# Dense row tiles of a two-layer graph kernel: eight by f32 matmuls, or ten by three bf16 parts

## The chip, the cores and the metric

The kernel runs on one core of one Trainium2 chip. The metric is the device time of one execution, in microseconds (us); a kernel's time is the median over its runs. The engines are named as the profile names them: PE (TensorE), DVE (VectorE), ACT (ScalarE), POOL (GpSimd) and SP (SyncE, which here only issues transfers). Each engine works through a queue of its own, in order. PSUM, into which PE accumulates, has eight banks of 128 x 512 f32 words; SBUF holds everything else that is on the core.

## The reference

`x` is 4096 x 512 in f32, `adj` a symmetric 0/1 matrix of 4096 x 4096 with ones on its diagonal and about nine in a row. Layer 0 is an attention in which every head takes the value of its best neighbour; layer 1, to which the change belongs, takes a mean over neighbours:

```python
def _L1_gnn_ref(x, adj, W_self, b_self, W_nb, b_nb, W_comb, b_comb):
    mask = (adj > 0).astype(x.dtype)
    deg = jnp.sum(mask, axis=1, keepdims=True)
    agg = mask @ x / jnp.maximum(deg, 1.0)
    self_f = x @ W_self + b_self
    nb_f = agg @ W_nb + b_nb
    combined = jnp.concatenate([self_f, nb_f], axis=-1)
    out = combined @ W_comb + b_comb
    return jax.nn.relu(out)

h = jnp.maximum(_layernorm(x, axis=-1), 0.0)
x = x + _L0_gnn_ref(h, adj, L0_gnn_WQ, ...)
h = jnp.maximum(_layernorm(x, axis=-1), 0.0)
x = x + _L1_gnn_ref(h, adj, L1_gnn_W_self, ...)
```

Matrices may be moved across the mean: with G = h · (W_nb · lower half of W_comb), a row's neighbour part is the sum of the rows of G that its mask picks, over its degree.

## The kernel before

`adj` is so sparse that the kernel turns it into lists. The first stage (to about 300 us) reads it, packs each row into bit words and computes keys and values. The rows are then sorted by degree into 32 tiles of 128 rows, the largest degrees first; `CAPS` gives the length of the lists in each tile (24, 15, 14, 13, 12, 12, 12, 11 | 11, 11, 10, ... 5), one entry of which is the row itself. `sidx` holds the lists, `perm` the place of each sorted row in the output. Should a list not fit, a flag (`fi`) makes the program run a general path afterwards; with these inputs it doesn't.

The middle stage goes through the tiles in 32 turns (`turns`, to about 905 us): attention, the second normalisation, and for each tile the row's own share (`X1_d`, rows of x and y) and its rows of G, stored to `G_d` by SP. Beside that, 105 one-hot rows are made here, one for each neighbour slot of the first DENSE = 8 tiles (`hots`): ACT makes each in two instructions (L1517, L1518) from codes that DVE computes (L1498), PE adds them up with the identity (`hot_product`), and `words_turn` turns each finished tile and stores it in `W_d` (L1549). The sum has, for row q and column c of 0 to 255, a word whose bit s says whether q has the neighbour 256·s + c; so one word covers the 16 planes of 256 rows of G. At the last turn `wT` is loaded with these words, 8 x 256 of 4 bytes in each partition (L1664). After the turns, ACT works off `owed_out` for rows owed from the middle stage and the tail.

The last stage, from the first gather of `G_d`, is what the change rewrites. It has two kinds of tiles.

Dense tiles, 0 to 7: PE multiplies masks with all 4096 rows of G, and each tile has a PSUM bank (`dacc`) to itself. For plane s, `dense_keys` (L1797) loads 256 rows of G into `gk` through SP, `dense_mask` (L1556) has DVE shift the words by 30 - s and keep bit 30, so that a neighbour reads 2.0 in f32 and all else 0, and `dense_sum` (L1805) issues 16 f32 matmuls of 128 x 512. The mask is made in two instructions, for seven tiles and for one; there are three mask buffers. The factor 2.0 is taken out by `half`, half of the reciprocal degree.

Sparse tiles, 8 to 31: for each neighbour slot POOL issues an indirect DMA that gathers 128 rows of `G_d` into `room` (L1121), n = CAPS - 1 for a tile, 174 in all. `room` is used as a ring of three tiles (L1863). DVE adds up the n rows in one tensor_reduce (`total`, L1830), for the last tile by pairwise additions (`halved`, L1839).

Either way `finish` follows: L1820 computes y + sum / degree, L1821 relu and x + that, two DVE instructions; y and x come from `X1_d` through SP, four tiles ahead (`load_x1`, L1813 and L1815). Then POOL stores the 128 rows to their places with an indirect DMA (`put_rows`, L1137); if two stores follow one another, a small memset (`gap`, L1136) goes between. The last stage's stores are issued one tile late: a tile's gathers come first, then the store of the tile before.

The order on all engines is the order of the code here (`manual_schedule`). The loop over sparse tiles counts POOL's calls, and plane s's mask, the load of keys s + 1 and the matmuls are issued once `calls >= pace * s - 7`, with `pace = 11`. The last three planes are issued together, tile by tile, so that the dense tiles become final one after another; `finish` of dense tiles 0 to 2 follows tile 29's, 3 to 5 tile 30's, and 6 and 7 stand ahead of the last sparse tile's:

```python
for k in (range(6, DENSE) if r == KT - 1 else ()):
    finish(k, dacc[k], half[:, k : k + 1], x1s.pop(k))
acc = (total if r < KT - 1 else halved)(gg, n)
finish(r, acc, smeta[:, r, M_RD - M_DEG : M_RD + 1 - M_DEG], x1s.pop(r))
for k in {KT - 3: range(0, 3), KT - 2: range(3, 6)}.get(r, ()):
    finish(k, dacc[k], half[:, k : k + 1], x1s.pop(k))
```

Of the kernel before, what the change touches and what calls it, by code (L numbers as in the profile page):

```python
# [9 lines left out]
F32 = mybir.dt.float32  # L10
BF16 = mybir.dt.bfloat16
I32 = mybir.dt.int32
# [6 lines left out]
P = 128  # L19
D = 512  # L20
# [497 lines left out]
GMAX = 10  # L518
DENSE = 8
# [25 lines left out]
def sparse_path(  # L545
# [14 lines left out]
    W_d = dram.tile([DENSE, P, 2, P], I32, tag="W_d", name="W_d")  # L560
# [550 lines left out]
    with ExitStack() as pb:  # L1111
# [379 lines left out]
        def word_codes(r):  # L1491

            n = CAPS[r] - 1
            code = bp.tile([P, 3, LIST], F32, tag="code", name="code")[:, :, 0:n]
            of = sidx[:, ds(sat[r] + 1, n)]
            ci = code[:, 2, :].bitcast(I32)
            nc.vector.tensor_scalar(ci, of, SEG - 1, None, ALU.bitwise_and)
            nc.vector.tensor_scalar(code[:, 0, :], ci, float(-STEEP), None, ALU.mult)  # L1498
            nc.vector.tensor_scalar(ci, of, 8, None, ALU.logical_shift_right)
            nc.vector.tensor_scalar(  # L1500
                code[:, 1, :].bitcast(I32), ci, float(2**23), float(127 * 2**23), ALU.mult, ALU.add
            )
            st[r]["code"] = code
# [35 lines left out]
        def words_turn():  # L1539

            for r, k, acc in summed:
                if k < CAPS[r] - 2:
                    continue
                pt = pst.tile([P, NC, P], F32, tag="tr", name="tr")
                for h in range(2):
                    nc.tensor.transpose(pt[:, h, :], st[r]["wg"][:, ts(h, P)], ident)
                wi = bp.tile([P, 2, P], I32, tag="wst", name="wi", bufs=1)
                nc.scalar.copy(wi, pt[:, 0:2, :])
                nc.sync.dma_start(W_d[r], wi)  # L1549
            summed.clear()  # L1550

        def dense_mask(s):

            mk = mks[s % 3]
            for a, b in ((0, DENSE - 1), (DENSE - 1, DENSE)):
                nc.vector.tensor_scalar(  # L1556
                    mk[:, a:b].rearrange("p r h q -> p r (h q)").bitcast(I32), wT[:, a:b, 0:SEG],
                    30 - s, 0x40000000, ALU.logical_shift_left, ALU.bitwise_and,
                )
            masks[s] = mk  # L1560
# [91 lines left out]
        for i in range(-5, KT):  # L1652
# [9 lines left out]
            if i == KT - 1:  # L1662
                wT = wp.tile([P, DENSE, SEG + 2], I32, tag="w_a", name="wT")
                nc.sync.dma_start(  # L1664
                    wT[:, :, 0:SEG], W_d.rearrange("r p h q -> p r (h q)")
# [110 lines left out]
        mks = [gp.tile([P, DENSE, 2, P], F32, tag="kg", name="mk") for _ in range(2)]  # L1776
# [6 lines left out]
    with ExitStack() as pd:  # L1783
# [5 lines left out]
        dacc = [psd.tile([P, D], F32, tag=f"da{r}", name="da") for r in range(DENSE)]  # L1789
        keys = {}  # L1790
        mks.append(kp.tile([P, DENSE, 2, P], F32, tag="mk", name="mk", bufs=1))
# [8 lines left out]
        def dense_sum(*planes):  # L1800
            todo = [(s, h, r) for s in planes for h in range(2) for r in range(DENSE)]
            if len(planes) > 1:
                todo.sort(key=lambda shr: shr[2])
            for s, h, r in todo:
                nc.tensor.matmul(  # L1805
                    dacc[r], masks[s][:, r, h, :], keys[s][:, h, :],
                    start=(s == 0 and h == 0), stop=(s == NPL - 1 and h == 1),
                )

        def load_x1(r):  # L1810
            x1 = dp.tile([P, 2, D], F32, tag="x1", name="x1", bufs=DENSE + 6)
# [14 lines left out]

        def total(g, n):

            acc = kp.tile([P, D], F32, tag="acc", name="acc", bufs=2)
            nc.vector.tensor_reduce(  # L1830
                acc, g[:, 0:n, :].rearrange("p n f -> p f n"), AX.X, ALU.add
            )
            return acc
# [16 lines left out]
        ahead, late3 = 2, NPL - 3  # L1850
        for s in range(ahead + 1):
            dense_keys(s)
        for s in range(ahead):
            dense_sum(s)
        s = ahead
        calls = 0

        pace = 11
        x1s = {}
        for r in range(DENSE, KT):  # L1860
            n = CAPS[r] - 1
            for q in [*range(r, min(r + 4, KT)), *(range(DENSE) if r == KT - 6 else ())]:
# [25 lines left out]
        assert s == NPL  # L1888
# [50 lines left out]
```

## Time and profile before

| | us |
|---|---|
| median of 3 runs (lowest, highest) | 1190.85 (1189.97, 1191.04) |
| the profiled execution | 1188.29 |
| its span, first to last instruction | 1186.5 |
| busy in the span: PE / DVE / ACT / POOL | 1023.9 / 982.7 / 550.1 / 715.1 |

The busy time of the engines in stretches of the last stage, with the TensorE clock that was granted in each (1.00 is full speed):

| stretch, us | PE | DVE | ACT | POOL | clock |
|---|---|---|---|---|---|
| 905 to 934 | 28.53 | 9.00 | 7.67 | 21.75 | 1.00 |
| 934 to 1000 | 65.80 | 60.89 | 0.15 | 50.25 | 1.00 |
| 1000 to 1060 | 60.00 | 57.70 | 0.00 | 45.68 | 1.00 |
| 1060 to 1122 | 56.44 | 55.62 | 0.00 | 47.37 | 1.00 |
| 1122 to 1151 | 28.37 | 26.06 | 0.00 | 20.86 | 0.89 |
| 1151 to 1173 | 12.60 | 20.29 | 0.00 | 16.33 | 0.84 |
| 1173 to 1186.5 | 0.00 | 0.00 | 0.00 | 0.00 | 0.50 |

A POOL busy time is that of the instructions themselves; the pause between two DMA issues is not in it. A group's line in the profile gives line, engine, operation, output and inputs, shape and count, then busy time and mean duration in ns, then the idle time before these instructions and what ended most of it. A timeline's line gives start, duration, engine, line, operation, operands and, in brackets, the wait before it and what ended that.

### The profile page before, as it was taken

To read this page: it belongs to the slowest core of one execution; us is meant where nothing else is said; L and a number is where in the kernel's file an instruction comes from. 1 tells how busy PE (TensorE), PEld (TensorE's weight loads), DVE (VectorE), ACT (ScalarE), POOL (GpSimd) and SP (SyncE) were. 2 spreads that over 40 slices of the span, in tenths; PEclk is the share of its full clock that TensorE was granted. 3 is DMA by queue.
4 is the path that set the end of the run, shared out by engine and by line. 5 is a ranking of instruction groups with operands and counts; after the bars stand their busy time and mean duration, and the time that the engine had idled before them with its cause. 6 is when DMAs were issued, how large, how long until landed. Compare 5 with 4: busy or idle time off the path is not lost. (4 is left out here: it accounts for less than half of the span.)

```text
span 1186.5 us, 11454 instructions
## 1 busy us (share of the span) xinstructions
PE 1023.9 (86%) x3079; PEld 501.6 (42%) x3079; DVE 982.7 (83%) x1548; ACT 550.1 (46%) x1222; POOL 715.1 (60%) x939
## 2 busy tenths in 40 slices
PE   3999999979599668688879989888989999999792
PEld 1555555644244224344334434444434444444340
DVE  4358789889289798798989999999983699998894
ACT  3777777932222377486567678754462100000000
POOL 3332323312677757757777777777713777777774
PEclk9999999989799878889889889888999999999996
DMA  9999999979797678889898889988865888888973
GB/s 353 418 420 418 413 418 375 396 226 293 229 269 251 180 233 261 255 278 292 281 289 281 284 280 298 291 279 280 284 256 171 306 310 275 321 288 276 369 242 108
DMA packets 115594, 348.44 MB, mean 294 GB/s; under 512 B 21472, under 2 KB 23552, under 8 KB 107328
## 3 DMA queue, kind: packets, MB, share of 16 engines
q0 software_dynamic: 60560, 201.01, 53.0%
q1 hardware_dynamic: 50560, 146.56, 32.5%
q10 hardware_dynamic: 4400, 0.05, 0.3%
q8 instruction: 26, 0.43, 0.1%
q14 instruction: 48, 0.39, 0.1%
HBM read 287.75 MB, written 64.00 MB: 296 GB/s over the span
## 5 line engine op out<-in xcount | busy, mean ns | idle before, releaser
L1805 PE MATMUL da<-gk,mk 128*128 128x512 f32 x512 | 223.2, 599 | 6.9 <-DVE mk L1556 6.2
L1121 POOL DMA_INDIRECT room<-G_d,sidx x174 | 168.5, 969 | 84.6 <-issue 80.7
L636 PE MATMUL q<-wq,hqT 128*128 128x512 f32 x256 | 151.0, 745 | 51.3 <-DVE pr L1244 51.3
L1250 DVE TENSOR_REDUCE sc<-pr 128x32 f32<-128x2048 f32 (+3 forms) x114 | 183.3, 1608 | 3.8
L1121 POOL DMA_INDIRECT kg<-K_d,sidx x161 | 153.4, 953 | 49.0 <-issue 40.2
L1830 DVE TENSOR_REDUCE acc<-room 128x512 f32<-128x4096 f32 (+5 forms) x23 | 153.0, 6651 | 32.5 <-DMA room<-G_d,sidx 30.6
L1805 PEld LDWEIGHTS da<-gk,mk 128*128 128x128 f32 x512 | 98.2, 192 | 131.9 <-issue 123.1
L1121 POOL DMA_INDIRECT room<-K_d,sidx x118 | 111.6, 945 | 42.9 <-issue 25.6
L1121 POOL DMA_INDIRECT o<-K_d,vi x112 | 108.1, 965 | 34.2 <-issue 32.0
L636 PE MATMUL pk<-wk,room 128*128 128x512 f32 x256 | 118.5, 606 | 2.6 <-ACT room L821 2.6
L636 PE MATMUL pv<-wv,room 128*128 128x512 f32 x256 | 112.6, 592 | 0.0
L636 PEld LDWEIGHTS q<-wq,hqT 128*128 128x128 f32 x256 | 59.2, 243 | 123.0 <-issue 77.7
L1244 DVE TENSOR_TENSOR pr<-q,kg 128x2048 f32<-128x2048 f32 (+3 forms) x47 | 93.3, 1985 | 11.2 <-DMA kg<-K_d,sidx 10.1
L1393 PE MATMUL pr<-swS,hT 128*128 128x512 f32 x216 | 97.1, 592 | 0.0
L636 PE MATMUL pg<-swN,hT 128*128 128x512 f32 x216 | 97.1, 593 | 0.0
L760 ACT ACTIVATE mkt<-adjt,sgb 128x2048 bf16<-128x2048 int32 x44 | 88.0, 1999 | 2.1 <-POOL adjt L678 2.1
L1244 DVE TENSOR_TENSOR pr<-q,room 128x2048 f32<-128x2048 f32 (+3 forms) x42 | 73.2, 1744 | 18.1 <-DMA room<-K_d,sidx 16.0
L636 PEld LDWEIGHTS pv<-wv,room 128*128 128x128 f32 x256 | 48.3, 190 | 59.3 <-issue 59.1
L636 PEld LDWEIGHTS pk<-wk,room 128*128 128x128 f32 x256 | 47.5, 196 | 51.5 <-issue 47.8
L830 DVE SCALAR_TENSOR_TENSOR ks<-pk,swe 128x512 f32<-128x512 f32 x32 | 21.9, 686 | 52.5 <-PE pk L636 46.8
L1517 ACT ACTIVATE hot<-ramp,code 128x256 bf16<-128x256 bf16 x105 | 52.5, 500 | 22.5 <-DVE code L1498 22.5
L779 PE MATMUL pw<-mkt,planes 128*128 128x256 bf16 x512 | 62.8, 277 | 0.0
(254 smaller groups left out, 1619.5 us busy)
## 6 DMA issues: line engine op xcount, KB each, us to landing
adjt<-adj_dram SPq DMA_DIRECT2D x44, 1024.0 KB, 10.4
room<-adj_dram SPq DMA_DIRECT2D x20, 1024.0 KB, 11.0
x<-X_d SPq DMA_DIRECT2D x25, 512.0 KB, 7.8
xt<-x_dram SPq DMA_DIRECT2D x32, 256.0 KB, 8.1
K_d<-ks POOLq DMA_DIRECT2D x32, 256.0 KB, 6.5
X_d<-xo SPq DMA_DIRECT2D x32, 256.0 KB, 4.5
G_d<-gs SPq DMA_DIRECT2D x32, 256.0 KB, 3.9
gk<-G_d SPq DMA_DIRECT2D x16, 512.0 KB, 4.8
```

The lines of the kernel that those rows point to most:

```text
L636: nc.tensor.matmul(dst, h[:, c, :], w[:, c, :], start=(c == 0), stop=(c == NC - 1))
L760: nc.scalar.activation(mk, st[t]["adj"][j], AF.Sigmoid, bias=sgb, scale=400.0, accum_out=degs[:, t, j : j + 1],)
L779: nc.tensor.matmul(pw, planes[:, s, :], st[t]["mk"][j][:, ts(i, SEG)], start=False, stop=(s == NPL - 1),)
L830: nc.vector.scalar_tensor_tensor(ks.rearrange("p (h d) -> p h d", h=H), st[t]["pk"].rearrange("p (h d) -> p h d", h=H), HD**-0.5, web.unsq ...
L1121: last[0] = nc.gpsimd.indirect_dma_start(out=dst, out_offset=None, in_=src, in_offset=bass.IndirectOffsetOnAxis(ap=idx, axis=0), element_o ...
L1244: nc.vector.tensor_tensor(pr[:, :g, :], s["q"].unsqueeze(1).to_broadcast([P, g, D]), kk[:, :, 0:D], ALU.mult)
L1250: nc.vector.tensor_reduce(sc[:, g0 : g0 + g, :], pr[:, :g, :].rearrange("p g (h d) -> p g h d", h=H), AX.X, ALU.add,)
L1393: nc.tensor.matmul(pr, s["hT1"][:, c, :], wS[:, c, :], start=False, stop=(c == NC - 1 and mine is None and not open_))
L1517: nc.scalar.activation(one, ramp, AF.Square, bias=code[:, 0, k : k + 1])
L1805: nc.tensor.matmul(dacc[r], masks[s][:, r, h, :], keys[s][:, h, :], start=(s == 0 and h == 0), stop=(s == NPL - 1 and h == 1),)
L1830: nc.vector.tensor_reduce(acc, g[:, 0:n, :].rearrange("p n f -> p f n"), AX.X, ALU.add)
```

## The change

Ten tiles are dense instead of eight, so 24 sparse tiles become 22, with 154 gathers. The ring's tiles become smaller (`GMAX` 9 rows instead of 10).

Each row of G is split by DVE into three bf16 parts that add up to it exactly (`dense_split`): the upper half of the f32 word as it stands, the upper half of what is left, and the remainder, written over the lower half of the word. PE reads these parts with a step of two bf16 words (4 bytes). A mask is now a bf16 2.0 or 0; the words are kept as 16 bits, in pairs, so that one DVE instruction on 1280 words of 4 bytes makes the masks of ten tiles and 256 rows. There are four mask buffers. For each tile and each block of two planes there are 12 bf16 matmuls of 128 x 512 (`dense_block`), 960 in all.

Seven dense tiles keep a bank of their own; tiles 7, 8 and 9 share the eighth. ACT copies each of their partial sums out, after each block, and DVE adds it to the tile's sum in SBUF (`add_part`). All sparse tiles are summed by `halved`; `total` is gone. Keys, masks, splits, blocks and additions are issued at places given in POOL calls (`events`, `START`, `PER`), also in the middle of a tile. The code of the one-hot rows covers 125 slots instead of 105, `W_d` and `wT` become half as wide for each tile, and the ring of `x1` has 11 tiles instead of 14. Lines below L1490 move: gathers are L1124, stores L1140, the mask L1558, the split L1811 and L1812, the matmuls L1827, the copy of a shared bank L1836, its addition L1844, `finish` L1863 and L1864, the halves L1874.

```diff
@@ -515,8 +516,10 @@
 FIRST = 4
-GMAX = 10
-DENSE = 8
+DENSE = 10
+GMAX = CAPS[DENSE] - 1
+BANKS = 7
+START, PER = 24, 19.5
 Q32 = 32
@@ -557,7 +560,7 @@
-    W_d = dram.tile([DENSE, P, 2, P], I32, tag="W_d", name="W_d")
+    W_d = dram.tile([DENSE, P, P], I32, tag="W_d", name="W_d")
     X1_d = dram.tile([N, 2, D], F32, tag="X1_d", name="X1_d")
@@ -1494,7 +1497,7 @@
             ci = code[:, 2, :].bitcast(I32)
-            nc.vector.tensor_scalar(ci, of, SEG - 1, None, ALU.bitwise_and)
+            nc.vector.tensor_scalar(ci, of, N | (SEG - 1), None, ALU.bitwise_and)
             nc.vector.tensor_scalar(code[:, 0, :], ci, float(-STEEP), None, ALU.mult)
@@ -1544,20 +1547,19 @@
                     nc.tensor.transpose(pt[:, h, :], st[r]["wg"][:, ts(h, P)], ident)
-                wi = bp.tile([P, 2, P], I32, tag="wst", name="wi", bufs=1)
-                nc.scalar.copy(wi, pt[:, 0:2, :])
-                nc.sync.dma_start(W_d[r], wi)
+                wi = bp.tile([P, SEG], U16, tag="wst", name="wi", bufs=1)
+                nc.scalar.copy(wi, pt[:, 0:2, :].rearrange("p h q -> p (h q)"))
+                nc.sync.dma_start(W_d[r], wi.bitcast(I32))
             summed.clear()
-            mk = mks[s % 3]
-            for a, b in ((0, DENSE - 1), (DENSE - 1, DENSE)):
-                nc.vector.tensor_scalar(
-                    mk[:, a:b].rearrange("p r h q -> p r (h q)").bitcast(I32), wT[:, a:b, 0:SEG],
-                    30 - s, 0x40000000, ALU.logical_shift_left, ALU.bitwise_and,
-                )
-            masks[s] = mk
+            mk = mks[s % 4]
+            nc.vector.tensor_scalar(
+                mk, wT, abs(14 - s), 0x40004000,
+                ALU.logical_shift_left if s < 15 else ALU.logical_shift_right, ALU.bitwise_and,
+            )
+            masks[s] = mk.bitcast(BF16)
@@ -1660,9 +1662,9 @@
             if i == KT - 1:
-                wT = wp.tile([P, DENSE, SEG + 2], I32, tag="w_a", name="wT")
+                wT = wp.tile([P, DENSE * P], I32, tag="w_a", name="wT")
                 nc.sync.dma_start(
-                    wT[:, :, 0:SEG], W_d.rearrange("r p h q -> p r (h q)")
+                    wT.rearrange("p (r q) -> p r q", q=P), W_d.rearrange("r p q -> p r q")
                 )
@@ -1773,7 +1775,9 @@
         assert not (hots or hot_now or summed)
-        mks = [gp.tile([P, DENSE, 2, P], F32, tag="kg", name="mk") for _ in range(2)]
+        mks = [gp.tile([P, DENSE * P], I32, tag="kg", name="mk") for _ in range(2)]
+        mks += [room[:, ds(KT * D - (k + 1) * DENSE * P, DENSE * P)].bitcast(I32) for k in range(2)]
         for k in range(2):
@@ -1786,9 +1790,9 @@
         order.enter_context(tc.manual_schedule())
-        dacc = [psd.tile([P, D], F32, tag=f"da{r}", name="da") for r in range(DENSE)]
-        keys = {}
-        mks.append(kp.tile([P, DENSE, 2, P], F32, tag="mk", name="mk", bufs=1))
+        dacc = [psd.tile([P, D], F32, tag=f"da{r}", name="da") for r in range(BANKS)]
+        sums = {}
+        keys, thirds = {}, {}
@@ -1797,18 +1801,57 @@
-        def dense_sum(*planes):
-            todo = [(s, h, r) for s in planes for h in range(2) for r in range(DENSE)]
-            if len(planes) > 1:
-                todo.sort(key=lambda shr: shr[2])
-            for s, h, r in todo:
-                nc.tensor.matmul(
-                    dacc[r], masks[s][:, r, h, :], keys[s][:, h, :],
-                    start=(s == 0 and h == 0), stop=(s == NPL - 1 and h == 1),
-                )
+        def dense_split(s):
+
+            gk = keys[s].rearrange("p h f -> p (h f)")
+            rest = kp.tile([P, 2 * D], F32, tag="rest", name="rest")
+            words = gk.bitcast(BF16).rearrange("p (x w) -> p x w", w=2)
+            high, low = words[:, :, 1], words[:, :, 0]
+            mid = rest.bitcast(BF16).rearrange("p (x w) -> p x w", w=2)[:, :, 1]
+            nc.vector.tensor_tensor(rest, gk, high, ALU.subtract)
+            nc.vector.tensor_tensor(low, rest, mid, ALU.subtract)
+            thirds[s] = (high, mid, low)
+
+        spread = list(range(BANKS))
+        for k, r in enumerate(range(BANKS, DENSE)):
+            spread.insert(3 * k, r)
+        to_add = []
+
+        def dense_block(b):
+            planes = (2 * b, 2 * b + 1)
+            todo = [(s, h, t) for s in planes for h in range(2) for t in range(3)]
+            for r in spread:
+                own = r < BANKS
+                acc = dacc[r] if own else psd.tile([P, D], F32, tag="da", name="da")
+                for s, h, t in todo:
+                    nc.tensor.matmul(
+                        acc, masks[s][:, ds((r * 2 + h) * P, P)], thirds[s][t][:, ts(h, D)],
+                        start=(s, h, t) == todo[0] and (b == 0 or not own),
+                        stop=(s, h, t) == todo[-1] and (b == NPL // 2 - 1 or not own),
+                    )
+                if not own:
+                    part = kp.tile(
+                        [P, D], F32, tag="sum" if b == 0 else "part", name="part", bufs=3
+                    )
+                    nc.scalar.copy(part, acc)
+                    if b == 0:
+                        sums[r] = part
+                    else:
+                        to_add.append((r, part))
+
+        def add_part(r):
+            part = next(p for q, p in to_add if q == r)
+            nc.vector.tensor_tensor(sums[r], sums[r], part, ALU.add)
+            to_add.remove((r, part))
+
+        def dense_total(r):
+            if r < BANKS:
+                return dacc[r]
+            add_part(r)
+            return sums[r]
         def load_x1(r):
-            x1 = dp.tile([P, 2, D], F32, tag="x1", name="x1", bufs=DENSE + 6)
+            x1 = dp.tile([P, 2, D], F32, tag="x1", name="x1", bufs=11)
             if r in owed or r in tail:
@@ -1823,14 +1866,6 @@
             put_rows(out[:, :], *done.pop(0))
-
-        def total(g, n):
-
-            acc = kp.tile([P, D], F32, tag="acc", name="acc", bufs=2)
-            nc.vector.tensor_reduce(
-                acc, g[:, 0:n, :].rearrange("p n f -> p f n"), AX.X, ALU.add
-            )
-            return acc
@@ -1847,19 +1882,38 @@
         puts.clear()
-        ahead, late3 = 2, NPL - 3
-        for s in range(ahead + 1):
+        for s in range(4):
             dense_keys(s)
-        for s in range(ahead):
-            dense_sum(s)
-        s = ahead
+        for s in range(2):
+            dense_split(s)
+        dense_block(0)
+        events = []
+        for b in range(1, NPL // 2):
+            at = START + PER * (b - 2)
+            for k in range(2):
+                s = 2 * b + k
+                if b > 1:
+                    events.append((at + PER + 1 + k, dense_keys, s))
+                events.append((at + PER + 6 + 5 * k if b > 1 else 8 + 8 * k, dense_mask, s))
+                events.append((at + PER + 6 + 5 * k if b > 1 else 8 + 8 * k, dense_split, s))
+            events.append((at + PER + 11 if b > 1 else 16, dense_block, b))
+        for b in range(1, NPL // 2 - 1):
+            for k, r in enumerate(range(BANKS, DENSE)):
+                events.append((START + PER * (b + (3 * k + 1) / DENSE) + 4, add_part, r))
+        events.sort(key=lambda e: e[0])
+
+        def progress(calls):
+            while events and events[0][0] <= calls:
+                _, step, arg = events.pop(0)
+                step(arg)
+
         calls = 0
-
-        pace = 11
         x1s = {}
+        turn_of = {KT - 2: spread[0:2], KT - 1: spread[2:]}
         for r in range(DENSE, KT):
             n = CAPS[r] - 1
-            for q in [*range(r, min(r + 4, KT)), *(range(DENSE) if r == KT - 6 else ())]:
+            more = {KT - 6: spread[0:4], KT - 3: spread[4:]}.get(r, ())
+            for q in [*range(r, min(r + 4, KT)), *more]:
                 if q not in x1s:
@@ -1868,24 +1922,16 @@
                 put()
-            for k in (range(6, DENSE) if r == KT - 1 else ()):
-                finish(k, dacc[k], half[:, k : k + 1], x1s.pop(k))
-            acc = (total if r < KT - 1 else halved)(gg, n)
-            finish(r, acc, smeta[:, r, M_RD - M_DEG : M_RD + 1 - M_DEG], x1s.pop(r))
-
-            for k in {KT - 3: range(0, 3), KT - 2: range(3, 6)}.get(r, ()):
-                finish(k, dacc[k], half[:, k : k + 1], x1s.pop(k))
+            if r == KT - 1:
+                for k in turn_of[r][0:3]:
+                    finish(k, dense_total(k), half[:, k : k + 1], x1s.pop(k))
+            progress(calls + n // 2)
+            finish(r, halved(gg, n), smeta[:, r, M_RD - M_DEG : M_RD + 1 - M_DEG], x1s.pop(r))
+            for k in turn_of.get(r, ())[3 * (r == KT - 1) :]:
+                finish(k, dense_total(k), half[:, k : k + 1], x1s.pop(k))
             calls += n + 1
-            while s < NPL and calls >= pace * s - 7:
-                dense_mask(s)
-                if s + 1 < NPL:
-                    dense_keys(s + 1)
-                if s < late3:
-                    dense_sum(s)
-                elif s == NPL - 1:
-                    dense_sum(*range(late3, NPL))
-                s += 1
+            progress(calls)
         while done:
         order.close()
```

More of the change, by code (lines that the diff above doesn't have):

```diff
@@ L11 @@
 BF16 = mybir.dt.bfloat16
+U16 = mybir.dt.uint16
 I32 = mybir.dt.int32
@@ L1775, in sparse_path @@
         assert not (hots or hot_now or summed)
-        mks = [gp.tile([P, DENSE, 2, P], F32, tag="kg", name="mk") for _ in range(2)]
+        mks = [gp.tile([P, DENSE * P], I32, tag="kg", name="mk") for _ in range(2)]
+        assert KT * D - 3 * GMAX * D >= 2 * DENSE * P
+        mks += [room[:, ds(KT * D - (k + 1) * DENSE * P, DENSE * P)].bitcast(I32) for k in range(2)]
         for k in range(2):
@@ L1870, in sparse_path @@
                 put()
-            for k in (range(6, DENSE) if r == KT - 1 else ()):
-                finish(k, dacc[k], half[:, k : k + 1], x1s.pop(k))
-            acc = (total if r < KT - 1 else halved)(gg, n)
-            finish(r, acc, smeta[:, r, M_RD - M_DEG : M_RD + 1 - M_DEG], x1s.pop(r))
-            for k in {KT - 3: range(0, 3), KT - 2: range(3, 6)}.get(r, ()):
-                finish(k, dacc[k], half[:, k : k + 1], x1s.pop(k))
-            calls += n + 1
-            while s < NPL and calls >= pace * s - 7:
-                dense_mask(s)
-                if s + 1 < NPL:
-                    dense_keys(s + 1)
-                if s < late3:
-                    dense_sum(s)
-                elif s == NPL - 1:
-                    dense_sum(*range(late3, NPL))
-                s += 1
-        assert s == NPL
+            if r == KT - 1:
[5 more added lines that the diff above has]
+                finish(k, dense_total(k), half[:, k : k + 1], x1s.pop(k))
+            calls += n + 1
+            progress(calls)
+        assert not events
         while done:
```

## The prediction

> **What bounds the kernel now.** I read the page's groups first, then the timelines of POOL, DVE and PE from 905 us on, since the diff leaves the stages before that nearly alone. The page gives the three candidates of the last stage:
>
> ```profile
> L1805 PE MATMUL da<-gk,mk 128*128 128x512 f32 x512 | 223.2, 599 | 6.9 <-DVE mk L1556 6.2
> L1121 POOL DMA_INDIRECT room<-G_d,sidx x174 | 168.5, 969 | 84.6 <-issue 80.7
> L1830 DVE TENSOR_REDUCE acc<-room 128x512 f32<-128x4096 f32 (+5 forms) x23 | 153.0, 6651 | 32.5 <-DMA room<-G_d,sidx 30.6
> ```
>
> POOL waits for nothing but "issue": 0.95 us of work and 0.30 us of pause, a gather each 1.25 us and a store of a tile's rows each 1.30 us. From the first gather (905.44) to the store at 1148.17, which follows the last gather of tile 30, stand 170 gathers and 20 stores: 170 × 1.25 + 20 × 1.30 = 238.5. The gathers' mean of 969 ns against their median of 946 adds 174 × 0.023 = 4.0. 905.44 + 242.5 = 1147.9, against 1148.17 seen: POOL's queue alone sets the pace up to there. From there DVE finishes the last tiles one after another, and the last store ends at 1172.98; 13.5 us of closing work follow to the end of the span.
>
> The 4.0 us are the key to this change. Gathers that are longer than 0.95 us stand beside DVE instructions that read two tiles in SBUF, and beside no others:
>
> ```profile
> 1082.87 6.33 DVE L1830 TENSOR_REDUCE acc<-room 128x512 f32<-128x3584 f32 x1 [1.77 <-DMA room<-G_d,sidx]
> 1088.79 1.00 POOL L1137 DMA_INDIRECT out_dram<-x,perm  x1 [0.30 <-issue]
> 1089.24 0.75 DVE L1820 SCALAR_TENSOR_TENSOR x<-acc,smeta,x 128x512 f32<-128x512 f32 x1
> 1090.02 0.69 DVE L1821 SCALAR_TENSOR_TENSOR x<-x 128x512 f32<-128x512 f32 x1
> 1090.10 1.45 POOL L1121 DMA_INDIRECT room<-G_d,sidx  x1 [0.30 <-issue]
> 1090.63 2.29 DVE L1556 TENSOR_SCALAR mk<-wT 128x1792 int32<-128x1792 int32 x2
> 1091.85 0.95 POOL L1121 DMA_INDIRECT room<-G_d,sidx  x1 [0.31 <-issue]
> ```
>
> The gather of 1090.10 took 0.50 too long. L1821 ended at 1090.71; had the gather to wait for that, its own need came at 1090.71 - 0.50 = 1090.21, 0.11 after its start. Beside L1830 and L1556 none grew. The same with additions of the kind that the change multiplies:
>
> ```profile
> 1168.28 1.94 DVE L1839 TENSOR_TENSOR room<-room 128x1024 f32<-128x1024 f32 x2
> 1168.64 1.70 POOL L1137 DMA_INDIRECT out_dram<-x,perm  x1 [0.31 <-DVE x L1821]
> ```
>
> The first of these two additions takes 1.22 (its row's longer form) and ends at 1169.50; a store that normally takes 0.97 to 1.00 took 1.70, so it waited from 1168.78 to 1169.50 and got in between the two. The gather of 1100.68 beside an L1820 of 1100.58 took 0.95: the lock begins some 0.2 into the DVE instruction. So I read: each POOL call needs one moment, 0.12 after its start; a DVE instruction with two SBUF inputs and duration T bars it from T = 0.2 to its end.
>
> **The change, part by part.**
>
> *POOL, removed.* Tiles 8 and 9 lose 10 gathers each, 20 × 1.25 = 25.0, and their 2 stores move to the end, 2.6. Up to tile 30 remain 150 × 1.25 + 18 × 1.30 = 210.9.
>
> *DVE, work.* Sums by halves: n rows take additions of (4,2,1,1), (4,2,1), (3,2,1), (3,1,1), (2,1,1) rows for n = 9 to 5. The row of L1244 gives 2.29, 1.76, 1.22 and 0.69 us for 2048, 1536, 1024 and 512 elements. With 4, 5, 5, 4, 3 tiles of n = 9 to 5 and one of 4 that is 9 × 2.29 + 9 × 1.76 + 18 × 1.22 + 33 × 0.69 = 81.2, in place of 153.0 + 1.9. Splits into thirds: 32 × 1.22 = 39.0. Adding the shared bank's parts: 21 × 0.69 = 14.5. Masks: 16 unbroken runs of 1280 words; per word the unbroken 768-word row L906 (528 ns) gives 0.88, the 1792-word row L1556 (2011 ns) 1.44; I take 0.88, the same layout, 14.1 in place of 37.2. In all 148.8 in place of 192.1: DVE has time to spare, but nearly all that is new reads two SBUF tiles, where L1830 read one.
>
> *DVE, what it does to POOL.* POOL calls come at least 1.25 apart. An instruction that bars for H = T - 0.2 costs H - 0.62 if H is over 1.25 (some call always meets it, at a random moment), else H × H / 2.5. That is 1.46 for 2.29, 0.94 for 1.76, 0.42 for 1.22, 0.10 for 0.69. An instruction of 1.22 that directly follows another barring one costs about nothing: the call got in at the seam, and the next is due 1.25 later, at its end. So up to tile 30: 9 × 1.46 = 13.1; 9 × 0.94 = 8.4; the first of each pair of splits, 16 × 0.42 = 6.7; the first addition of the n = 5 tiles, 3 × 0.42 = 1.3; 32 + 18 short ones × 0.10 = 4.8; together 34.3, less 0.6 for tile 30's own, 33.7. Without the credit for seams 14 additions and 16 second splits more cost 12.5: the upper end. Masks: no gather beside the 256-word masks grew by more than 0.07, so I take 0; barring like the others (H = 0.68) they would cost 14 × 0.18 = 2.6. The lower end, each barring instruction costing no more than an L1820/L1821 pair does now (4.0 for 20 tiles, 0.2 a pair), is 21 tiles and 16 splits × 0.2 = 7.
>
> The Trainium skill ("SBUF — State Buffer", section "Who interferes with whom") reports a probe in which tensor_copy stalled GpSimd's DMA but tensor_tensor and tensor_reduce did not, and infers that descriptor generation does not need the read interface. The store at 1168.64 says otherwise for an indirect DMA. By the probe the halves would cost POOL nothing and the time would be that of the first rival below; the measurement decides.
>
> *POOL path and tail.* 905.44 + 210.9 + 33.7 + 3.6 (18 of the 20 old pairs' waits) = 1153.6 is the end of tile 30's gathers; the last starts at 1152.4 and lands 5.0 later (median of the tile's view), 1157.4. Then DVE: tile 30 (2.7 and 1.5), ten dense tiles × 1.40 (the spacing of L1820/L1821 pairs), three adds × 0.7, tile 31 (1.9 and 1.5): 23.7, to 1181.1. One more store, 1.2: 1182.3, against 1172.98: +9.3.
>
> *PE.* 960 bf16 matmuls of 512 columns in place of 512 f32 passes of 0.43. The last bf16 one of that width:
>
> ```profile
> 901.78 0.39 PE L1391 MATMUL pr<-sbb,s 96*128 96x512 bf16 x1
> 902.00 3.60 PE L1393 MATMUL pr<-swS,hT 128*128 128x512 f32 x8
> ```
>
> 0.22 from start to start; sixteen 256-wide ones (L779) in 1.91 give 0.109 each, 0.218 doubled, with their 99-ns weight loads hidden. 960 × 0.218 = 209, 26.2 per block of two planes. The start stays at 934.2 (it waits for ACT's last copy): the four splits of planes 0 and 1 run from about 915, when the keys have landed (issue at 910.19 + 4.8), inside the 22 us in which DVE now idles before 923.52. A block's time on POOL is 19.5 calls × (1.26 + 0.2) = 28.5, so PE waits for splits and not the reverse. Plane 15 is split before tile 28's sum, some 40 us before the last dense tile is finished; PE needs 26 of them. New for it: the moving operand steps by 4 bytes. No row shows that for bf16; the ends are 0.22 and the f32 pass, 0.43, which also reads 4 bytes a column. I take the bf16 row. That page ("Door 1: The DMA port swizzle") says that strides within a 16-byte line run at full rate, which would keep 0.22.
>
> *ACT* copies the shared bank 24 × 0.58 us on an engine idle since 934; a bank has two tiles (5.2 us) before it is needed again. *SP*: the same 16 key loads, now two per block behind a wait for PE, with X1 loads behind them; those are issued four tiles (some 40 calls, 55 us) ahead. Were that gone, a tile's finish would wait one landing, 5 to 9 us. The mask and split behind a full mask buffer wait on PE's block b - 2, done by then.
>
> *Earlier stages.* 20 more one-hot rows fall into turns 24 to 27. Pairs of turns with and without them are at hand: 31.9 and 32.1 us with (20 to 23), 31.2 and 32.1 without (24 to 27). Two pairs × 0.35 = +0.7; ends -0.4 and +1.8.
>
> Sum: +9.3 + 0.7 = +10 on the profiled execution (1188.29 us, span 1186.5); on the median of 1190.85 that is **1201 us**.
>
> **Rivals.** (1) *No lock for additions: faster.* If POOL's waits stay at 3.6, tile 30's gathers end at 1119.9, data are there at 1123.7, DVE ends at 1147.4, after PE (934.2 + 209 = 1143). With the store 1148.6: -24.4 + 0.7, **1167 us**. For it speaks 25.0 us of calls that are really gone; against it the 1.70. It decides if waits stay below 24 us; between lie a few outcomes of no change. (2) *PE becomes the bound: slower.* From (1180 - 934) / 960 = 0.256 us a matmul on, PE ends last. At 0.43: 934.2 + 413 + 3 = 1350, +177, **1368 us**. Against it the bf16 rows. (3) *Waits without the credit for seams, masks barring too*: 12.5 + 2.6 more, **1216 us**; for it speaks that DVE often idles between pieces, so that phases are random. (4) The change misses its point if PE falls back behind its plan and DVE stands at an add of a part, its queue of sums behind it; POOL's ring of three tiles would then stop. With 26.2 against 28.5 us a block it doesn't come to that.
>
> **How the numbers follow.** Slower by POOL's waits, with (3) as its upper part: 0.70. (2): 0.04. (1), with anything clearly faster: 0.18. No change: 0.08. 0.2% (2.4 us) is about what a measurement can tell from none. So faster 0.18, same 0.08, slower 0.74. The likeliest case's own range is 1190 to 1216; taking in the near side of no change, and a little for unequal landings, 1183 to 1217 leaves out (2) and most of (1).
>
> **What would show it.** Gathers of room with a mean near 1.17 us in place of 0.97, the long ones beside L1874 and L1811, ending when these do; POOL still never idle until tile 30's gathers, about 1154; DVE less than 150 us in sums, splits, adds and masks; matmuls L1827 0.22 apart, with gaps on PE that end on splits; the last store near 1182. Wrong if gathers beside L1874 keep 0.95 (then 1167), or if matmuls are over 0.256 apart.

## The result, and the profile after

The changed kernel takes 1209.76 us (median of 4 runs, 1207.79 to 1213.53) against 1190.41 for the kernel before in the same comparison: a ratio of 1.0169, 95% interval 1.0141 to 1.0196. It is slower by 19.4 us, where some 10 were forecast. The profiled execution took 1209.33 us, its span is 1207.4.

The groups of the changed kernel's page, with the lines that answer to those of before (count, busy time, mean ns of one, idle time before):

```profile
L1124 POOL DMA_INDIRECT room<-G_d,sidx x154 | 187.8, 1220 | 80.0 <-issue 76.9
...
L1874 DVE TENSOR_TENSOR room<-room 128x512 f32<-128x512 f32 (+3 forms) x69 | 81.3, 1178 | 72.5 <-DMA room<-G_d,sidx 60.6
...
L1827 PE MATMUL da<-gk,mk 128*128 128x512 bf16 x313 | 99.2, 394 | 10.9 <-DVE mk L1558 8.9
```

The gathers are 20 fewer and cost more together: 187.8 us against 168.5, 1220 ns each against 969. The halves take 81.3 us of DVE, and DVE idles 60.6 us waiting for gathered rows; before, it idled 30.6 so. The bf16 matmuls stand 0.226 us apart (median from start to start of the 940 of 960 that the trace holds; the 394 ns are modelled durations of overlapping matmuls).

Where the calls wait is seen in the timeline of DVE and POOL (start, duration, engine, line):

```profile
943.00 1.29 POOL L1124 DMA_INDIRECT room<-G_d,sidx  x1 [0.30 <-DVE x L1863]
943.35 0.82 DVE L1558 TENSOR_SCALAR room<-wT 128x1280 int32<-128x1280 int32 x1
944.09 1.22 DVE L1811 TENSOR_TENSOR rest<-gk 128x1024 f32<-128x1024 f32 x1
944.60 1.60 POOL L1140 DMA_INDIRECT out_dram<-x,perm  x1 [0.30 <-issue]
945.34 1.38 DVE L1812 TENSOR_TENSOR gk<-rest 128x1024 bf16<-128x1024 f32 x1
946.50 3.22 POOL L1124 DMA_INDIRECT room<-G_d,sidx  x1 [0.30 <-issue]
946.60 5.00 DVE L1874 TENSOR_TENSOR room<-room 128x2048 f32<-128x2048 f32 x4
950.03 0.95 POOL L1124 DMA_INDIRECT room<-G_d,sidx  x1 [0.30 <-issue]
```

A normal call takes 0.95 (gather) or 0.99 us (store), and needs its moment 0.12 after its start, as the prediction read. The gather of 943.00 needs it at 943.12 and has 0.34 too much: that is 943.46, the end of L1864, which began at 942.74. The store of 944.60 waits to the end of the first subtraction (944.09 + 1.22 = 945.31). The gather of 946.50 comes while the second subtraction still runs (to 946.72); the first of four additions starts at 946.60, before that end, and takes 2.29. The gather ends at 949.72, which is 0.83 after 948.89: it waited for both and got in after the first of the four additions. So it goes all along. From 900 to 1166 us, 78 of 169 calls are more than 0.05 too long, and all 78 are freed within 0.05 us of the end of a DVE instruction.

In stretches of the last stage (length; busy time and count of instructions of PE, PEld, which is PE's weight loads, DVE, ACT and POOL; then the granted clock, the busy share of the DMA engines and GB/s):

```profile
1000.00:1060.00 60.00, 56.19 (x233) 23.38 (x239) 43.12 (x44) 3.52 (x6) 47.96 (x40) 0.92 0.71 225
1060.00:1122.00 62.00, 57.61 (x240) 23.71 (x243) 45.78 (x49) 3.52 (x6) 50.05 (x40) 0.94 0.80 270
...
1173.00:1195.00 22.00, 1.87 (x8) 0.64 (x7) 21.01 (x30) 0.00 (x0) 13.58 (x25) 0.66 0.45 163
```

From 1060 to 1122 DVE is busy 45.78 of 62 us, against 55.62 before, and POOL 50.05 against 47.37 for fewer instructions (40 against 49). The work that DVE saved became idle time, and the time that POOL saved became waiting.

### The profile page after: what moved, and what is told of

The parts are those of the page before. It is cut to its first block, busy times and chain, and to the rows that moved or that the text cites. A ratio compares the mean times of both kernels' runs of the same rounds, so it can differ in the third digit from the quotient of the medians.

```text
span 1207.4 us, 12538 instructions
## 1 busy us (share of the span) xinstructions
PE 1026.1 (85%) x3535; PEld 498.9 (41%) x3555; DVE 939.8 (78%) x1637; ACT 583.2 (48%) x1292; POOL 739.7 (61%) x921
## 4 chain that ended last, share of the span: by engine, by line
PE 27%; DVE 21%; DMA 20%; POOL 18%; issue 10%; ACT 3%; POOLq 0%; DVEq 0%; ACTq 0%
POOL room L1124 10%; PE pk L639 7%; DVE pr L1247 6%; PE pv L639 6%; DMA room<-G_d,sidx 5%; DVE sc L1253 5%; DMA room<-K_d,sidx 4%; PE q L639 4%; DMA kg<-K_d,sidx 4%; PE pw L782 3%; PE pr L1396 3%; POOL kg L1124 2%; POOL out_dram L1140 2%; POOL o L1124 2%; DVE o L1293 2%
## 5 line engine op out<-in xcount | busy, mean ns | idle before, releaser
L1124 POOL DMA_INDIRECT room<-G_d,sidx x154 | 187.8, 1220 | 80.0 <-issue 76.9
L1124 POOL DMA_INDIRECT kg<-K_d,sidx x161 | 153.6, 954 | 49.7 <-issue 39.0
L1124 POOL DMA_INDIRECT room<-K_d,sidx x118 | 111.8, 948 | 44.7 <-issue 24.4
L1874 DVE TENSOR_TENSOR room<-room 128x512 f32<-128x512 f32 (+3 forms) x69 | 81.3, 1178 | 72.5 <-DMA room<-G_d,sidx 60.6
L1124 POOL DMA_INDIRECT o<-K_d,vi x112 | 107.7, 961 | 34.1 <-issue 32.6
L1836 ACT COPY part<-da 128x512 f32<-128x512 f32 x24 | 14.1, 587 | 215.8 <-PE da L1827 185.7
L1827 PE MATMUL da<-gk,mk 128*128 128x512 bf16 x313 | 99.2, 394 | 10.9 <-DVE mk L1558 8.9
L1247 DVE TENSOR_TENSOR pr<-q,kg 128x2048 f32<-128x2048 f32 (+3 forms) x47 | 93.3, 1985 | 13.5 <-DMA kg<-K_d,sidx 9.9
L1827 PE MATMUL da<-gk,room 128*128 128x512 bf16 x313 | 98.9, 393 | 3.7 <-DVE room L1558 2.6
L1247 DVE TENSOR_TENSOR pr<-q,room 128x2048 f32<-128x2048 f32 (+3 forms) x42 | 73.2, 1743 | 15.1 <-DMA room<-K_d,sidx 10.0
L1827 PEld LDWEIGHTS <-mk 128*128 128x128 bf16 x480 | 46.5, 97 | 76.5 <-DVE mk L1558 9.4
L1827 PEld LDWEIGHTS <-room 128*128 128x128 bf16 x480 | 46.5, 97 | 68.8 <-issue 5.9
L1520 ACT ACTIVATE hot<-ramp,code 128x256 bf16<-128x256 bf16 x125 | 62.5, 500 | 22.8 <-DVE code L1501 22.8
```

What stands on the lines that cost most here:

```text
L1124: last[0] = nc.gpsimd.indirect_dma_start(out=dst, out_offset=None, in_=src, in_offset=bass.IndirectOffsetOnAxis(ap=idx, axis=0), element_o ...
L1247: nc.vector.tensor_tensor(pr[:, :g, :], s["q"].unsqueeze(1).to_broadcast([P, g, D]), kk[:, :, 0:D], ALU.mult)
L1520: nc.scalar.activation(one, ramp, AF.Square, bias=code[:, 0, k : k + 1])
L1827: nc.tensor.matmul(acc, masks[s][:, ds((r * 2 + h) * P, P)], thirds[s][t][:, ts(h, D)], start=(s, h, t) == todo[0] and (b == 0 or not own) ...
L1874: nc.vector.tensor_tensor(g[:, 0:h, :], g[:, 0:h, :], g[:, n - h : n, :], ALU.add)
```

## The experiments

Chips differed. The chip of a_reduce, b_halved, a_nosplit and b_hots10, and that of b_halved_2, b_hots10_2, a_mix3 and a_mix2, held PE back for long stretches: the kernel before itself took 1477 and 1472 us there, its mean granted clock was about 0.85 instead of 0.93, and in the runs on these two chips the first gather of the last stage starts at 1114 to 1126 us instead of 905. These times can't be set against the 1190 us of the other chips. The lengths of POOL's calls could still be read.

How the waits are summed, here and below: for each call of POOL in the last stage, up to the last store, what it took over 0.945 (gather) or 0.99 (store) if that is over 0.05, laid onto the DVE instructions that ran from 0.12 after its start on; where two overlap, onto the earlier one. By this the kernel before has 4.5 us, the changed one 46.8 (44.7 up to 1166).

**a_reduce**: the sums of the changed kernel by tensor_reduce, for all sparse tiles but the last. `total` is put back for this, with its results in the spare ends of two mask buffers. In this run and the a_mix runs the lines named above lie 2 further on (L1813 and L1814 the split, L1846 the addition of a part, L1865 and L1866 `finish`), `total` is L1875 and the halves are L1884.

```diff
-            finish(r, halved(gg, n), smeta[...], x1s.pop(r))
+            finish(r, (total if r < KT - 1 else halved)(gg, n), smeta[...], x1s.pop(r))
```

> The changed kernel with the sums of all sparse tiles but the last by one tensor_reduce over the rows again (one SBUF input) in place of additions by halves. Theory (additions with two SBUF inputs bar POOL's gathers): of the 45 us by which POOL's calls up to tile 30 are longer than normal, the 27 beside the halves (L1874) vanish, the mean gather falls from 1.22 to about 1.05 us, tile 30's gathers end near 1138 instead of 1165. DVE has 56 us more work, so its own queue then comes close to being the limit: 1185 to 1196 us. Rival (gathers are longer for another reason, such as the traffic of the bf16 matmuls or of the key loads): gathers stay at about 1.2 us and the time is 1205 us or more.

Measured: the waits are 17.0 us, the mean gather 1.024 us, and not one call was held by a tensor_reduce. The ratio to before is 0.985 (0.9814 to 0.9885) on a chip that held PE back, so the expected times were not tested; the rival's gathers of 1.2 us are refuted.

**b_halved, b_halved_2, b_halved_3**: the halves alone, in the kernel before.

```diff
-            acc = (total if r < KT - 1 else halved)(gg, n)
+            acc = halved(gg, n)
```

> The kernel before with all sparse tiles summed by halves, nothing else of the change. Theory: with the waits per addition that the changed kernel's trace shows (1.53 us for 2048 elements, 1.03 for 1536, about 0.1 for the short ones, 2.0 for the 2560 elements of the two tiles with ten rows) POOL's calls take some 33 us more; DVE has about 70 us less work, which buys nothing; 1215 to 1224 us, and calls with up to 2 us too much ending with an addition. Rival (no barring; DVE's work counts): the tail gets 2 us shorter and the time is 1186 to 1190 us.

> The kernel before with all sparse tiles summed by halves, once more, since the first run's chip held PE back for long stretches and its times say little of POOL. Theory: POOL's calls take 33 us more (seen there), DVE's tail is 2 us shorter: a ratio to before of 1.022 to 1.029. Rival (DVE's freed 70 us pay for part of it): below 1.015.

> The kernel before with all sparse tiles summed by halves, on a chip of its own call. The two runs so far had PE held back on their chips for long stretches, so that PE and not POOL set the end; the waits of POOL's calls were 36 to 38 us there, against 4. Theory for a chip that doesn't hold PE back: 33 us more on POOL's path, 2 us less in DVE's tail: a ratio to before of 1.022 to 1.029. Rival (DVE's freed 70 us pay for part of it): below 1.015. On a chip that holds PE back: near 0.975 again.

Measured: the waits are 37.6, 36.4 and 34.2 us. On the two chips that held PE back the ratios are 0.9725 (0.9691 to 0.9759) and 0.9758 (0.9716 to 0.9801): both expectations of time missed, and their signs too; why the halves are faster there stays open. On the third chip (before: 1189.63) it is 1215.9 us, 1.0234 (1.0209 to 1.0259), inside what the theory said. The groups of that third run:

```profile
L1121 POOL DMA_INDIRECT room<-G_d,sidx x174 | 197.2, 1133 | 84.7 <-issue 81.0
...
L1839 DVE TENSOR_TENSOR room<-room 128x512 f32<-128x512 f32 (+4 forms) x77 | 92.3, 1199 | 112.6 <-DMA room<-G_d,sidx 79.2
```

The same 174 gathers take 197.2 us in place of 168.5, beside additions that cost DVE 92.3 us where the sums had cost 153.0 + 1.9. One line of code costs 26.3 us, more than the whole change's 19.4, with f32 matmuls and eight dense tiles.

**a_nosplit**: no subtractions. The middle and lower parts of G are left out, and the upper part is multiplied three times.

```diff
-            nc.vector.tensor_tensor(rest, gk, high, ALU.subtract)
-            nc.vector.tensor_tensor(low, rest, mid, ALU.subtract)
-            thirds[s] = (high, mid, low)
+            thirds[s] = (high, high, high)
```

> The changed kernel without the splits: all three matmuls of a row pair read the upper bf16 part of G, and DVE makes no parts (the computation left out is the two subtractions per plane). PE's work is the same. Theory: the 8.0 us of POOL waits beside L1811 and L1812 vanish and with them some of the waits that began under a split and went on under an addition: 1198 to 1203 us. Rival (splits matter by holding up PE or by DVE's time): PE's gaps before matmuls shrink but the time stays within 3 us of 1209.

Measured: the waits are 30.4 us, 16.4 less than in the changed kernel; 8.0 of these are the subtractions' own; 4.8 are fewer waits beside the halves and 2.4 beside the additions of parts, though both do the same work as before (chips differ, too). The ratio to before, 0.9747 (0.9709 to 0.9786), is from a chip that held PE back, on which the changed kernel itself was not measured: what the subtractions cost in time stays untested.

**b_hots10, b_hots10_2, b_hots10_3**: the words of two more tiles, made and stored, but not used.

```diff
-        hots = [(r, k) for r in range(DENSE) for k in range(CAPS[r] - 1)]
+        hots = [(r, k) for r in range(10) for k in range(CAPS[r] - 1)]
```

> The kernel before that makes the one-hot rows and words of ten tiles instead of eight in the middle stage, and uses eight. Theory (the 20 one-hot rows more delay the last turns): the first gather of the last stage moves from 905.4 to about 908.8, as in the changed kernel, 1193 to 1195 us. The prediction's size of this term: 1191. Rival (the 3.4 us are a difference between single executions, or come of the uint16 words): 1190.4 and a first gather near 905.4.

> The kernel before that makes the one-hot rows and words of ten tiles and uses eight, once more for the same reason. Theory: the first gather of the last stage moves from 905.4 to about 908.8 us and the ratio is 1.002 to 1.004. The prediction's term of 0.7 us: 1.0006. Rival (the 3.4 us come of another part): 1.000 and a first gather near 905.4.

> The kernel before that makes the one-hot rows and words of ten tiles and uses eight, in a call of its own. Theory: the first gather of the last stage moves from 905.4 to about 908.8 us and the ratio is 1.002 to 1.004, on a chip that doesn't hold PE back. The prediction's term of 0.7 us: 1.0006. Rival (the 3.4 us come of another part of the change): 1.000 and a first gather near 905.4.

Measured: 1.0033 (1.0013 to 1.0052) and 1.0022 (0.9983 to 1.006) on the two chips that held PE back; on the third 1.0003 (0.9993 to 1.0012), with the first gather at 906.9. My theory falls there: on that chip the 20 one-hot rows cost at most 1.4 us. In the six executions on chips that did not hold PE back the first gather starts at 905.4 (before), 904.2 (b_halved_3), 906.9, 908.8 (changed), 908.8 (a_mix) and 905.5 (a_mix3_2); kernels with equal middle stages differ by 3.3, so most of the 3.4 us of the changed kernel's profile can be scatter. What causes the scatter wasn't found.

**a_mix, a_mix3, a_mix2, a_mix3_2**: tensor_reduce for the early tiles, halves for the last five, three or two.

```diff
-            finish(r, halved(gg, n), smeta[...], x1s.pop(r))
+            finish(r, (total if r < KT - 5 else halved)(gg, n), smeta[...], x1s.pop(r))
```

> The changed kernel with one tensor_reduce for the sums of tiles 10 to 26 and additions by halves only for the last five tiles, where DVE's own queue sets the end and not POOL's calls. Theory (the loss of the changed kernel is the barring of POOL's calls by additions): POOL's calls up to tile 30 are about 19 us longer than normal instead of 45 to 47, and the time is 10 to 14 us below the changed kernel's 1.0169 of before: a ratio of 1.005 to 1.009. Rival (barring matters, but the changed kernel is held by the rest of the change too: DVE's queue, PE's plan, the middle stage): the ratio stays above 1.012. If the sums were all, and DVE had room, it would be below 1.000.

Measured: 1187.44 us against 1188.16, 0.9988 (0.9975 to 1.0001), where 1.005 to 1.009 were expected: a larger gain than the theory asked. My estimate had let DVE's longer queue take back half. Of the changed kernel's waits 24.7 us are left, and the last store ends at 1176.6 instead of 1195.9, after the same first gather at 908.8. DVE still had room near the end (timelines of POOL and of DVE in a_mix):

```profile
1128.43 2.73 POOL L1124 DMA_INDIRECT room<-G_d,sidx  x1 [0.30 <-issue]
...
1136.28 2.85 POOL L1140 DMA_INDIRECT out_dram<-x,perm  x1 [0.30 <-issue]
```

```profile
1145.25 0.69 DVE L1866 SCALAR_TENSOR_TENSOR gs<-gs,x 128x512 f32<-128x512 f32 x1
1151.77 2.68 DVE L1884 TENSOR_TENSOR room<-room 128x1024 f32<-128x1024 f32 x3 [5.83 <-DMA room<-G_d,sidx]
```

Two calls that met the halves of tiles 27 and 28 (the second also the end of L1814 and an addition of a part) took 1.78 and 1.86 us too long, and then DVE stood for 5.83 us before tile 30's sum, because its rows came late. Hence:

> The changed kernel with tensor_reduce for tiles 10 to 28 and halves for the last three. In a_mix DVE stood idle for 5.8 us before tile 30's sum, waiting for gathers that POOL had issued late behind the halves of tiles 27 to 29. Theory: two tiles more by tensor_reduce give DVE 4 us more work inside that idle time and POOL 3 to 4 us less of waits: 0.995 to 0.998 of before. Rival (DVE's own work sets the end by now): 0.999 to 1.002.

> The same with halves for the last two tiles only. Theory: one more tile's waits of 1 to 2 us go, DVE has 2 us more: equal to a_mix3 within 0.15%. Rival (DVE's queue sets the end): 0.2% slower than a_mix3.

> The changed kernel with tensor_reduce for tiles 10 to 28 and halves for the last three, in a call of its own. In a_mix (0.9988) DVE stood idle for 5.8 us before tile 30's sum, waiting for gathers that POOL had issued late behind the halves of tiles 27 to 29. Theory, on a chip that doesn't hold PE back: two tiles more by tensor_reduce give DVE 4 us more work inside that idle time and POOL 3 to 4 us less of waits: 0.995 to 0.998 of before. Rival (DVE's own work sets the end by now): 0.999 to 1.002.

Measured on the second chip that held PE back: a_mix3 0.9832 (0.9788 to 0.9876) and a_mix2 0.9825 (0.9791 to 0.9859), not to be told apart. On a chip that did not, a_mix3_2 took 1185.67 us against 1189.34: 0.997 (0.9958 to 0.9982), a little faster than the kernel before, 2% faster than the changed one by their ratios, and in the range of the theory. Its groups in the last stage:

```profile
L1124 POOL DMA_INDIRECT room<-G_d,sidx x154 | 159.6, 1036 | 78.3 <-issue 76.2 <-DMA room<-G_d,sidx 0.9 <-DMA out_dram<-x,perm 0.6
L1875 DVE TENSOR_REDUCE mk<-room 128x512 f32<-128x4096 f32 (+4 forms) x19 | 127.6, 6714 | 2.5 <-DMA room<-G_d,sidx 2.5
...
L1884 DVE TENSOR_TENSOR room<-room 128x512 f32<-128x512 f32 (+1 forms) x8 | 7.2, 894 | 0.2
```

154 gathers take 159.6 us (1036 ns each), and the sums cost DVE 127.6 + 7.2 us instead of 81.3. DVE does 53 us more in sums than in the changed kernel, and the kernel is 2% faster. Waits: 20.2 us.

## Why the prediction came out as it did

*The lock: right, and nearly right in size.* The forecast of 1201 us was 8.8 us short: the direction and the cause were foretold, and POOL's waits were priced too low. The prediction's prices per instruction against the sums of the changed kernel's trace, from 900 to 1166 us:

| DVE instruction | count | foretold each | foretold, us | measured, us |
|---|---|---|---|---|
| additions of 2048 (L1874) | 9 | 1.46 | 13.1 | 13.7 |
| additions of 1536 (L1874) | 9 | 0.94 | 8.4 | 9.3 |
| additions of 1024 (L1874) | 16 | 0.42 for 3 of them | 1.3 | 1.7 |
| first subtraction (L1811) | 16 | 0.42 | 6.7 | 6.6 |
| second subtraction (L1812) | 16 | 0 | 0 | 1.4 |
| additions of 512 (L1874, L1844) | 48 | 0.10 | 4.8 | 4.8 |
| masks (L1558) | 14 | 0 | 0 | 1.8 |
| pairs of `finish` | 20 | 0.2 | 3.6 | 5.3 |

With the 0.6 taken off for tile 30's own additions, 37.3 were foretold up to tile 30's gathers, and 44.7 came. Of the 7.4 between them, 4.9 are terms set to nothing or left at their old price: masks 1.8, pairs of `finish` 1.7, second subtractions 1.4. The additions of 2048 and 1536, a little over their prices, make 1.5 more.

"An instruction of 1.22 that directly follows another barring one costs about nothing: the call got in at the seam" held for the most part: without this credit 12.5 us more were foretold, and 1.8 of these came (the 1.4, and 0.4 for additions of 1024). In the changed kernel's trace a waiting call got in at all 55 boundaries between barring instructions at which the second starts after the first ends (0.03 after, as L1812 after L1811, where the store of 944.60 got in). Where the second starts earlier, the overlap matters: the gather of 943.00 got in at the end of L1864 though the mask had started 0.08 before, and the gather of 946.50 did not at the end of L1812, where the first addition had started 0.12 before. With overlaps up to 0.084 calls got in at 16 of 18 boundaries, with 0.091 to 0.130 at 1 of 10; nine of these ten are ends of L1812. So a seam is lost mostly behind the second subtraction.

"Masks: no gather beside the 256-word masks grew by more than 0.07, so I take 0" priced the time of the new mask by one row and its lock by another. The old mask of 1792 words takes 2.01 us, 1.12 ns a word; the new one takes 0.82 for 1280, 0.64 ns a word, and it bars:

```profile
1001.19 0.82 DVE L1558 TENSOR_SCALAR mk<-wT 128x1280 int32<-128x1280 int32 x1
1001.67 1.16 POOL L1124 DMA_INDIRECT room<-G_d,sidx  x1 [0.31 <-issue]
1001.94 1.21 DVE L1811 TENSOR_TENSOR rest<-gk 128x1024 f32<-128x1024 f32 x1
```

The call needs its moment at 1001.79, the mask ends at 1002.01, and the call is 0.22 too long. (Here, too, it got in though L1811 starts 0.07 before that end.) The Trainium skill ("SBUF — State Buffer", section "Who interferes with whom") says that a tensor_scalar can enter a faster mode that uses the port pair shared with GpSimd; the two masks agree with that. Its inference from a probe, that tensor_tensor leaves descriptor generation alone, does not hold for the indirect DMAs here: 27.0 of b_halved_3's 34.2 us of waits lie on tensor_tensor additions. The prediction left out that the same section has a DVE instruction with two SBUF inputs contend with a GpSimd instruction that reads SBUF. That would fit if the waiting call reads its indices (`sidx`, in SBUF); no run here tests it.

*POOL's path.* 908.8 (first gather) + 210.9 (calls) + 45.3 (all excess) = 1165.0, where the store after tile 30's gathers starts, at 1165.03. Foretold were 1153.6 from a start of 905.4, with 0.7 more for the middle stage apart. Of the difference 8.0 us are waits, and 3.4 are the later start, 2.7 more than the 0.7; the experiments do not lay this start on the change.

*The tail.* 28.7 us were foretold from there to the end of the last store; it took 30.9 (1165.0 to 1195.9). The closing work took 11.5 instead of 13.5. That these two cancel is luck; the runs don't show why either moved. 2.7 + 8.0 + 2.2 - 2.0 = 10.9, nearly all of the 11.0 between the 1198.3 foretold and the 1209.33 measured for the profiled execution.

*PE and DVE.* 0.226 us a matmul against 0.218 foretold: the step of 4 bytes costs a bf16 operand next to nothing. The waits view of the changed kernel (total, times, longest):

```profile
DVE room L1874 <- DMA room<-G_d,sidx: 60.6, 13, 7.5
...
PE da L1827 <- DVE mk L1558: 8.9, 1, 8.9
```

PE stood 8.9 us for one mask, and as foretold it waits for DVE and not DVE for PE; but its gaps were foretold to end on splits, and 2.7 us of them do, against 11.5 on masks. The halves took 81.3 us (foretold 81.2), the subtractions 41.2 (39.0; a second one takes 1.36 instead of 1.22) and the additions of parts 14.3 (14.5).

*The rivals.* No lock for additions (1167) fell with gathers like that of 946.50. PE as the bound (1368) fell with 0.226. Waits without the credit for seams and with masks barring (1216) came nearest to the measured 1209.76 by luck: of the 15.1 us that it adds, 3.6 came (1.8 of 12.5 for seams, 1.8 of 2.6 for masks), and the rest of the gap has the other causes above. DVE did not stand at an `add_part` for PE.

## What to carry to other kernels

Before an engine is given cheaper instructions, ask what they lock: in b_halved_3 63 us less of DVE work cost 26 us, because POOL's queue set the pace and the cheaper form reads two SBUF tiles. Here tensor_reduce, which reads one SBUF tile, was the better form while POOL was the bound, and the shorter form only in the tail, where DVE was (a_mix3_2). One SBUF input alone is no guarantee: the new mask has one, and it bars. Price such a lock by the length of the instruction: long ones cost far more than the same time in short ones (1.53 us for one of 2.29, 0.10 for one of 0.69).

## What the runs showed of the hardware

What bars POOL's indirect DMAs can be counted over six traces (the two kernels, a_mix, a_mix3_2, b_halved_3, b_hots10_3). Taken are the calls of the last stage whose moment, 0.12 after their start, lies at least 0.22 after the start of a DVE instruction and 0.06 before its end; a call over 0.05 too long counts as held.

| DVE instruction | calls held |
|---|---|
| tensor_tensor, both inputs in SBUF | 160 of 160 |
| `finish`, both tiles in SBUF | 109 of 109 |
| `finish`, one tile in PSUM | 0 of 35 |
| tensor_reduce, one input in SBUF | 0 of 407 |
| mask of 1280 words (0.64 ns a word) | 15 of 15 |
| mask of 1792 words (1.12 ns a word) | 0 of 61 |

The same instruction of `finish` bars or not by where its inputs lie. In the tail of a_mix:

```profile
1155.88 0.68 DVE L1846 TENSOR_TENSOR part<-part 128x512 f32<-128x512 f32 x1
1156.24 1.18 POOL L1140 DMA_INDIRECT out_dram<-gs,perm  x1 [0.78 <-DVE gs L1866]
...
1157.99 0.74 DVE L1865 SCALAR_TENSOR_TENSOR x<-da,half,x 128x512 f32<-128x512 f32 x1
1158.35 0.97 POOL L1140 DMA_INDIRECT out_dram<-x,perm  x1 [0.82 <-DVE x L1866]
```

The store of 1156.24 is 0.2 too long, to the end of L1846 (two SBUF operands); that of 1158.35 needs its moment at 1158.47, in the middle of an L1865 that reads `da` from PSUM, and takes the normal 0.97.

On two chips PE is held back. In b_hots10 such a stretch looks so (PE's timeline, then two windows, columns as above):

```profile
1213.17 1.01 PE L1805 MATMUL da<-gk,mk 128*128 128x512 f32 x1 [1.09 <-issue]
1215.97 1.01 PE L1805 MATMUL da<-gk,mk 128*128 128x512 f32 x1 [1.79 <-issue]
1218.78 1.01 PE L1805 MATMUL da<-gk,mk 128*128 128x512 f32 x1 [1.79 <-issue]
```

```profile
1196.00:1205.00 9.00, 9.00 (x22) 3.99 (x21) 8.96 (x4) 0.00 (x0) 6.87 (x8) 1.00 0.68 204
1207.00:1227.00 20.00, 8.08 (x8) 2.07 (x8) 1.91 (x1) 0.00 (x0) 12.22 (x13) 0.53 0.62 185
```

From 1196 to 1205 there are 22 matmuls in 9 us, from 1207 to 1227 eight in 20 us, at a granted clock of 0.53, with nothing waited for that the profile shows. There the order of kernels turns round: the halves alone were 2.4 to 2.8% faster than before, with the granted clock at 0.93 in the last stage of b_halved against 0.87 in b_hots10, which differs from the kernel before only by the added words. Whether less work on DVE lets PE run more freely was not tested.
